# A fused convolution-as-attention and state-space kernel: C products dealt out by sixteen-part patterns, a clip moved from GpSimd into a relu, and tables of hooks reordered

## The chip, the cores and the metric

The kernel runs on one core of a Trainium2 chip. A core has five engines that each run their own list of instructions in order and wait for each other through semaphores: TensorE (PE, with its weight loads shown apart as PEld), VectorE (DVE), ScalarE (ACT), GpSimd (POOL) and SyncE (SP), which here issues the transfers (DMA). The metric is the device time of one execution, in microseconds (us), as the median of three runs.

## The reference

`x` has shape (8, 256, 48, 48), that is 8 images of 256 channels and N = 2304 pixels ("tokens"), in float32. Two layers are added to it, each behind a group norm. The first finds for each pixel the 16 most similar pixels and averages their features; the second is a two-deep chain of selective state-space ("mamba") blocks that scan over the pixels.

```python
# layer 0, per image
feat_pos = tokens @ W.T + bias                      # 256 features, 256 position channels
pos = pos / maximum(norm(pos), 1e-12)
sim = einsum('bnc,bmc->bnm', pos, pos)              # 2304 x 2304
topksim, topkid = top_k(sim, 16)
out = einsum('bnk,bnkc->bnc', softmax(topksim), feat[topkid])
x = x + out
# layer 1, twice (DEPTH = 2), per image: D_INNER = 512, D_STATE = 16, D_CONV = 4
xn = layernorm(xf)
xi, z = split(xn @ in_w.T)
xc = silu(causal_conv4(xi))
dt_r, B, C = split(xc @ xp_w.T)
dt = softplus(dt_r @ dtp_w.T + dtp_b)
# for every pixel t in order:
h = h * exp(dt_t * A) + dt_t * B_t * x_t            # h: 512 x 16 per image
y_t = sum over the 16 states of h * C_t
y = (y + xc * D) * silu(z)
x = x + y @ out_w.T                                 # after the second block
```

## The kernel before

The pixels of an image go in chunks of T = 384, so there are 6 chunks x 2 blocks = 12 *units* per image and 96 in all, one after the other. A unit holds 16 *steps* of 32 inner channels, laid out so that 128 partitions hold 32 channels x 4 groups of states; the other 4 states lie along the free axis. A step has two *parts* of two states each. So a unit has 32 parts, and every part has one scan on VectorE.

A step costs: `make_bx` (GpSimd, dt times x times B, two steps ahead), four `decay` exponentials (ScalarE, into one of two PSUM banks, one part ahead), two scans (VectorE), and the product of the state with C. That product is done by one of two engines, part by part. `on_pool` says which. In a "V" part VectorE makes it, straight after the scan, from the bank `da`; ScalarE then saves the last state and clears a column (`carry`) before the bank is filled again. In a "G" part the scan writes into `bx` and GpSimd makes the product one step later (`pool_part`); if both parts of a step are GpSimd's, one instruction covers them. PE sums the states of four steps (`sum_states`).

```python
    PARTS = Q // HQ            # 2
    STEPS = DI // G            # 16
    HOOKS = PARTS * STEPS      # 32 parts in a unit
    LEAD = 2
    BLOCK = 16
    TOPK = (1, 10)
    PHASE = 6
    # ... cut ...
    def decays(m):
        return banks[m % 2][:, 511 - T : 513 + T]

    def on_pool(unit, i, p):
        if unit["b"] + 1 == B:
            return p == PARTS - 1 and i % J < J - 1
        if TOPK[0] <= unit["at"] < TOPK[1]:
            return p == PARTS - 1 or i % 2 == 0
        return p == PARTS - 1

    def run_scan(m):
        # ... cut ...
        h = g if on_pool(unit, i, p) else da
        nc.vector.tensor_tensor_scan(h, da, g, 0.0, ALU.mult, ALU.add)
        if h is da:
            nc.vector.tensor_tensor(
                bx[:, :, 0:T], da.rearrange("p (q t) -> p q t", q=HQ)[:, :, 1:],
                unit["BC"][1][:, qs], ALU.mult,
            )

    def carry(m):
        # ... cut ...
        if not on_pool(unit, i, p):
            h = decays(m).rearrange("p (q t) -> p q t", q=HQ)
            if unit["c"] + 1 < NCH:
                nc.scalar.copy(h_st[:, unit["d"], i, p * HQ : (p + 1) * HQ], h[:, :, T])
            nc.scalar.copy(h[:, :, 0], zeros)

    def pool_part(n):
        # ... cut ...
        lo = [p for p in range(PARTS) if on_pool(unit, i, p)]
        if not lo:
            return
        qs = slice(lo[0] * HQ, (lo[-1] + 1) * HQ)
        g = unit["bx"][i][:, qs]
        nc.gpsimd.tensor_tensor(g[:, :, 0:T], g[:, :, 1:], unit["BC"][1][:, qs], ALU.mult)
```

The second block of a chunk follows two chunks behind the first. All other work of a unit (layer norm, input projection, the four taps of the convolution, loads, gates, output projection) hangs on the parts by two tables: `between` is called before the scan of a part, `behind` after it, and the number in front is the part, counted from the unit's first (negative ones lie in the units before it). The similarity search of the *next* image runs beside the units as one more stream, `layer0`, that gives a little work per part. Its projections fill the first unit of an image, its blocks of 128 pixels the next nine (16 parts a block), by a third table, `within`. The last image has no such stream.

```python
    for m in range(PARTS * NSTEP - HOOKS + end + 1):
        # ... cut ...
        carry(m - 1)
        decay(m + 1)
        if p == 0:
            make_bx(n + LEAD)
            pool_part(n - 1)
            take_up(n + 1)
        else:
            carry_pool(n - 1)
        for f, unit, args in inner.get(m, ()):      # the table "between"
            f(unit, *args)
        run_scan(m)
        for f, unit, args in outer.get(m, ()):      # the table "behind"
            f(unit, *args)
        # ... cut: then one piece of layer0 of the next image
```

In that stream the norm of the position channels is clipped and turned into its inverse root, by ScalarE's logarithm and exponential and a Newton step on GpSimd:

```python
        def inverse_norm(c):
            rn[c] = small.tile([P, TB], F32, tag="rn", name=f"rn_{b}_{c}")
            rsqrt_start(rn[c], n2[c], 0.0)                                  # ScalarE: Ln, Exp
            rsqrt_end(nc.gpsimd, rn[c], n2[c], 0.0, f"rn_{b}_{c}")          # GpSimd: Newton

            def norm(pn):
                n2[c] = small.tile([P, TB], F32, tag="n2", name=f"n2_{b}_{c}")
                nc.scalar.copy(n2[c], pn)

                nc.gpsimd.tensor_scalar(n2[c], n2[c], 1e-24, None, ALU.max)
```

Of the kernel before, what the change touches and what calls it, by code (L numbers as in the profile page):

```python
# [8 lines left out]
F32 = mybir.dt.float32  # L9
BF16 = mybir.dt.bfloat16  # L10
AF = mybir.ActivationFunctionType
ALU = mybir.AluOpType
# [3 lines left out]
P = 128  # L16
GSIZE = 8
TAKEN = -4.0
FAR = 64.0


@with_exitstack
def tile_conv_preact(
# [18 lines left out]
    nc = tc.nc  # L42
    B, C, N = x.shape
# [11 lines left out]
    G = 32  # L55
    J = P // G
# [3 lines left out]
    PARTS = Q // HQ  # L60
# [4 lines left out]
    BLOCK = 16  # L65
    TOPK = (1, 10)
    PHASE = 6
    JR = 1
    assert N % T == 0 and N % P == 0 and T % P == 0 and NS % (J * HQ) == 0

    const = ctx.enter_context(tc.tile_pool(name="const", bufs=1))
# [13 lines left out]
    nc.vector.tensor_scalar(minus, ident, -FAR, None, ALU.mult)  # L85
    three = const.tile([P, 1], F32, tag="three", name="three")
    nc.gpsimd.memset(three, 3.0)
    ones_mean = const.tile([P, P], F32, tag="ones_mean", name="ones_mean")
    nc.gpsimd.memset(ones_mean, 1.0 / C)
    ones_col = const.tile([P, 1], F32, tag="ones_col", name="ones_col")  # L90
# [60 lines left out]
    def rsqrt_start(r, var, eps):  # L151

        nc.scalar.activation(r, var, AF.Ln, bias=eps)
        nc.scalar.activation(r, r, AF.Exp, scale=-0.5)
# [66 lines left out]
    def layer0(b, left, pool, ps0, alone):  # L221
# [37 lines left out]
        n2, rn = {}, {}  # L259
# [11 lines left out]

        def inverse_norm(c):
            rn[c] = small.tile([P, TB], F32, tag="rn", name=f"rn_{b}_{c}")
            rsqrt_start(rn[c], n2[c], 0.0)
            rsqrt_end(nc.gpsimd, rn[c], n2[c], 0.0, f"rn_{b}_{c}")

        def scale(c):

# [9 lines left out]
        def chunk(c, xn):  # L288
            cs = slice(c * T, (c + 1) * T)
            sq = []  # L290

            def project(ob):
                pp = mm0(T, f"pp_{b}_{c}_{ob}")
                for k in range(CB):
                    nc.tensor.matmul(
                        pp, w0_sb[:, k, C + ob * P : C + (ob + 1) * P], xn[:, k, :],
                        start=(k == 0), stop=(k == CB - 1),
                    )
                return pp

            def features(j):
                pf = mm0(C, f"pf_{b}_{c}_{j}")
                for k in range(CB):
                    nc.tensor.matmul(
                        pf, xn[:, k, j * P : (j + 1) * P], w0_sb[:, k, 0:C],
                        start=(k == 0), stop=(k == CB - 1),
                    )
                return pf

            def norms():  # L310
                pn = mm0(TB, f"pn_{b}_{c}")
                for j in range(TB):
                    for k in range(CB):
                        nc.tensor.matmul(
                            pn[:, j : j + 1], sq[0][:, k, j * P : (j + 1) * P], ones_col,
                            start=(k == 0), stop=(k == CB - 1),
                        )
                return pn

            def position(ob):  # L320
                def use(pp):
                    nc.scalar.activation(
                        pos[:, ob, cs], pp, AF.Identity, bias=b_pos[:, ob : ob + 1]
                    )
                    if ob == CB - 1:
                        sq.append(
                            pool.tile([P, CB, T], F32, tag="x", name=f"sq_{b}_{c}", bufs=3 * more)
                        )
                        nc.scalar.activation(sq[0], pos[:, :, cs], AF.Square)

                return use

            def feature(j):
                return lambda pf: nc.scalar.copy(feat[:, c * TB + j, :], pf)

            def norm(pn):
                n2[c] = small.tile([P, TB], F32, tag="n2", name=f"n2_{b}_{c}")
                nc.scalar.copy(n2[c], pn)

                nc.gpsimd.tensor_scalar(n2[c], n2[c], 1e-24, None, ALU.max)  # L340

            for ob in range(CB):
                step(lambda: project(ob), position(ob))
                yield
            if c > 0:
                inverse_norm(c - 1)
            step(lambda: features(0), feature(0))
            yield
            if c > 0:
                scale(c - 1)  # L350
                yield
            for j in range(1, TB):
                step(lambda: features(j), feature(j))
                yield
            step(norms, norm)

        xn = normalized(0)
# [114 lines left out]
        def finish(t):  # L472
# [11 lines left out]


        within = [
            (15, turn, 1), (11, others, 1), (-8, similar, 1), (-2, keep_similar, 3), (-6, keep_similar, 1),
            (-5, keep_similar, 2), (24, turn_back), (19, weights, 3), (1, top, 1), (16, weigh, 0),
            (-9, similar, 0), (-8, similar, 2), (-9, keep_similar, 0), (22, average), (-5, similar, 4),
            (4, top, 3), (-6, similar, 3), (-3, keep_similar, 4), (0, top, 0), (5, others, 0),  # L490
            (3, top, 2), (7, add_top), (5, others, 2), (11, others, 3), (7, others, 4),
            (14, turn, 0), (17, turn, 2), (15, weights, 0), (17, turn, 3), (15, weights, 1),
            (20, turn, 4), (18, weights, 2), (19, weigh, 1), (21, weigh, 3), (10, invert),
            (19, weigh, 2), (20, weights, 4), (21, weigh, 4), (24, finish),
        ]
        begin = min(part for part, *_ in within)
# [14 lines left out]
    with tc.tile_pool(name="first", bufs=1) as pool0, tc.tile_pool(  # L511
        name="first_ps", bufs=1, space=PSUM
# [234 lines left out]
    def silu_z(unit):  # L747
# [3 lines left out]
        for e in range(DB - 1):  # L751
# [11 lines left out]
             dt=[], dt_d={}, dtx_d={}, dtr={}, dtxr={}, bx={}, y={}, inw={}, dmat={}, taps={}, xi={}, cv={},  # L763
# [8 lines left out]

    def on_pool(unit, i, p):

        if unit["b"] + 1 == B:
            return p == PARTS - 1 and i % J < J - 1
        if TOPK[0] <= unit["at"] < TOPK[1]:
            return p == PARTS - 1 or i % 2 == 0
        return p == PARTS - 1

    def make_bx(n):

# [115 lines left out]
    def leave(unit, cb):  # L898
# [14 lines left out]


    between = [
        (-41, load_v), (-32, variance), (7, in_proj, 5), (17, sum_states, 1), (-21, in_proj, 0),
        (38, out_proj, 0), (-16, in_proj, 3), (-15, taps, 2), (-10, softplus), (24, sum_states, 2),
        (-5, load_rep, "dt", 0), (-11, step_size, 0), (-33, center), (18, load_rep, "dtx", 13), (-21, tap, 0),
        (2, load_rep, "dtx", 5), (-17, tap, 1), (-23, load_in, 1), (-17, tap, 2), (-28, load_in, 2),
        (-16, load_in, 7), (19, gate, 1), (-9, times_x, 1), (-8, load_rep, "dtx", 0), (-4, load_rep, "dtx", 2),  # L920
        (25, load_rep, "dt", 15), (-2, load_rep, "dtx", 3), (1, load_rep, "dt", 3), (0, load_rep, "dtx", 4), (4, load_rep, "dtx", 6),
        (7, load_rep, "dt", 6), (10, load_rep, "dtx", 9), (13, load_rep, "dt", 9), (33, sum_states, 3), (15, load_rep, "dt", 10),
        (5, load_rep, "dt", 5), (17, load_rep, "dt", 11), (20, load_rep, "dtx", 14), (5, load_d, 1), (20, load_d, 2),
        (-33, square), (-15, load_in, 5), (-22, load_in, 0), (21, load_rep, "dt", 13), (-11, step_size, 1),
        (11, load_rep, "dt", 8), (8, in_proj, 6), (-32, root), (9, copy_z, 2), (11, gate, 0),
        (38, out_proj, 1), (-6, load_rep, "dtx", 1), (-4, load_bc, 1), (6, in_proj, 7), (3, in_proj, 4),
        (-13, x_proj), (16, load_rep, "dtx", 12), (-2, times_x, 3), (-11, load_in, 6), (-35, affine),
        (39, leave, 0), (-30, spread_root), (23, load_rep, "dt", 14), (-3, load_rep, "dt", 1), (2, times_x, 2),
        (-16, taps, 1), (-14, taps, 3),
    ]  # L930
    behind = [
        (39, leave, 1), (-32, root_end), (-26, load_in, 3), (-1, load_rep, "dt", 2), (28, gate, 2),
        (6, load_rep, "dtx", 7), (9, load_rep, "dt", 7), (12, load_rep, "dtx", 10), (14, load_rep, "dtx", 11), (-12, split),
        (8, load_rep, "dtx", 8), (-18, in_proj, 2), (-15, load_in, 4), (3, load_rep, "dt", 4), (29, load_d, 3),
        (-14, silu_x), (35, gate, 3), (-35, mean), (-20, taps, 0), (-23, normal),
        (22, load_rep, "dtx", 15), (-15, tap, 3), (-20, in_proj, 1), (-28, scale), (-10, load_bc, 0),
        (10, sum_states, 0), (7, copy_z, 0), (5, load_d, 0), (9, silu_z), (19, load_rep, "dt", 12),
        (8, copy_z, 1), (-10, times_x, 0), (33, load_out),
    ]
    inner, outer, early = {}, {}, []  # L940
    for w, unit in enumerate(units):
# [16 lines left out]
    for m in range(PARTS * NSTEP - HOOKS + end + 1):  # L958
        n, p = divmod(m, PARTS)
# [69 lines left out]
```

## Time and profile before

| what | value |
|---|---|
| time, median of 3 runs | 10485.8 us (10466.35 to 10491.26) |
| profiled execution, span | 10473.1 us |
| mean granted TensorE clock | 0.853 |
| one scan, VectorE | 1.75 us |
| top-k passes, VectorE, four per block of 128 pixels, 144 blocks | 2.54 to 2.55 us each |
| transfers | 1271.49 MB, mean 121 GB/s |

A page of the profile names a group of instructions by its line in the kernel, the engine, the operation, and output<-inputs with their shapes; then the busy time of the group in us, the mean duration of one in ns, and after the second bar the idle time of the engine just before them with what ended it. "L857" is line 857 of the kernel. The answers on waits read: engine, line and tile that waited <- what it waited for: us in total, times, longest. A window line gives start and end, the length, and each engine's busy time with the number of instructions. "issue" is time in which the engine waited for nothing that the profile shows.

### The profile page before, as it was taken

The numbers are of one execution on the slowest core, as the hardware profiler recorded it, in microseconds if no ns is written. First come the engines' busy times: TensorE is split into PE (matmuls) and PEld (weight loads), VectorE is DVE, ScalarE is ACT, GpSimd is POOL, SyncE is SP. The second block draws the span as 40 slices with busy tenths as digits, with TensorE's granted clock in tenths as the row PEclk, the third lists the DMA queues.
The fourth block names the chain that finished last, engine by engine and source line by source line (L and its number), as shares of the span: only waits on it lengthen the run. The fifth ranks groups of instructions, "written<-read, shape, count | busy, mean of one in ns | idle before, by whom it ended". The sixth has DMA issues, their size and how long they took to land.

```text
span 10473.1 us, 135567 instructions
## 1 busy us (share of the span) xinstructions
PE 8225.8 (79%) x36736; PEld 4471.3 (43%) x36736; DVE 9041.7 (86%) x8040; ACT 7506.5 (72%) x17226; POOL 8918.0 (85%) x4142
## 2 busy tenths in 40 slices
PE   8788886888868887788877888678886888866555
PEld 6544443444434444344433444344443444422222
DVE  4589997899979999799987999879998899988898
ACT  4477776777767777677776777767776777766766
POOL 0189997999979999799997999879998899988887
PEclk9888987898878888889887989789897888877777
DMA  1144444444444444444444444444444444444444
GB/s 31 55 111 126 123 131 127 122 123 127 125 134 119 123 126 128 129 120 126 123 129 120 131 125 126 129 123 120 129 127 137 113 128 119 133 130 121 135 132 115
DMA packets 1243516, 1271.49 MB, mean 121 GB/s; under 512 B 266592, under 2 KB 1215840, under 8 KB 1242752
## 3 DMA queue, kind: packets, MB, share of 16 engines
q1 hardware_dynamic: 1230496, 1262.45, 44.3%
q8 instruction: 294, 4.82, 0.2%
q14 instruction: 470, 3.85, 0.1%
q10 hardware_dynamic: 12256, 0.36, 0.1%
HBM read 1048.94 MB, written 212.86 MB: 120 GB/s over the span
## 4 chain that ended last, share of the span: by engine, by line
PE 29%; ACT 25%; DVE 21%; DMA 9%; SPq 9%; issue 6%; POOL 2%; ACTq 0%; DVEq 0%; POOLq 0%
ACT da L812 10%; SPq L559 7%; DVE bx L827 6%; PE psim L385 6%; DVE da L827 5%; PE po L451 5%; DMA dtxr<-dtx_d 4%; PE pe L585 4%; PE y L875 3%; DVE bx L829 2%; PE pw L893 2%; PE pt L431 2%; DVE xc L685 2%; ACT sim L394 2%; DMA dtr<-dt_d 1%
## 5 line engine op out<-in xcount | busy, mean ns | idle before, releaser
L788 POOL TENSOR_TENSOR bx<-BC,dtxr 128x1536 f32<-128x1536 f32 x1536 | 5296.6, 3449 | 268.9 <-PE y L875 190.4
L812 ACT ACTIVATE da<-dtr,A_sb 128x384 f32<-128x384 f32 x6144 | 3585.3, 584 | 630.6 <-DVE bx L827 441.1
L827 DVE TENSOR_TENSOR_SCAN bx<-da,bx 128x770 f32<-128x770 f32 x1992 | 3452.7, 1748 | 283.2 <-ACT da L812 267.8
L857 POOL TENSOR_TENSOR bx<-bx,BC 128x1536 f32<-128x1536 f32 (+1 forms) x1488 | 3260.6, 2191 | 371.3 <-DVE bx L827 273.2
L827 DVE TENSOR_TENSOR_SCAN da<-da,bx 128x770 f32<-128x770 f32 x1080 | 1893.5, 1753 | 251.0 <-ACT da L812 123.4
L385 PE MATMUL psim<-pos 128*128 128x512 f32 (+1 forms) x2880 | 1482.9, 649 | 455.7 <-ACT sim L394 212.4
L585 PE MATMUL pe<-vn,inw 128*128 128x384 f32 (+1 forms) x3072 | 1244.6, 536 | 259.9 <-DMA inw<-in_in_wT_dram 106.8
L451 PE MATMUL po<-feat,aT 128*128 128x256 f32 x5184 | 1315.9, 407 | 1.0
L875 PE MATMUL y<-bx,sel 128*32 128x384 f32 x12288 | 1245.5, 539 | 46.7 <-POOL bx L857 27.5
L451 PEld LDWEIGHTS po<-feat,aT 128*128 128x128 f32 x5184 | 1032.7, 203 | 299.7 <-issue 107.2
L829 DVE TENSOR_TENSOR bx<-da,BC 128x768 f32<-128x768 f32 x1080 | 1035.4, 959 | 37.9 <-DMA BC<-bc_d 0.9
L385 PEld LDWEIGHTS psim<-pos 128*128 128x128 f32 x2880 | 573.2, 212 | 1143.3 <-issue 470.9
L585 PEld LDWEIGHTS pe<-vn,inw 128*128 128x128 f32 x3072 | 609.4, 208 | 727.2 <-issue 178.9
L685 DVE SCALAR_TENSOR_TENSOR xc<-pe,cw,xc 128x384 f32<-128x384 f32 x1152 | 704.4, 612 | 87.5 <-ACT xc L677 60.2
L875 PEld LDWEIGHTS y<-bx,sel 128*32 128x32 f32 x12288 | 391.3, 119 | 899.3 <-issue 764.3
L440 ACT ACTIVATE aT<-pt 128x512 f32<-128x512 f32 (+1 forms) x720 | 396.4, 551 | 489.5 <-PE po L451 269.0
L715 PE MATMUL pd<-dbl,dtp_sb 16*128 16x384 f32 x768 | 443.1, 693 | 306.3 <-ACT dt L724 169.2
L431 PE MATMUL pt<-ident,sim 128*128 128x128 f32 x2592 | 577.2, 307 | 80.7 <-ACT aT L440 39.4
L394 ACT COPY sim<-psim 128x512 f32<-128x512 f32 (+1 forms) x720 | 383.1, 532 | 317.8 <-PE psim L385 316.7
L872 PE MATMUL y<-xc,dmat 128*128 128x384 f32 x768 | 413.5, 627 | 208.8 <-ACT bx L802 108.3
L893 PE MATMUL pw<-z,ow 128*128 128x384 f32 x1536 | 546.1, 510 | 34.5 <-DMA ow<-in_out_wT_dram 10.7
L735 POOL TENSOR_TENSOR dtx<-dt,xc 128x384 f32<-128x384 f32 x384 | 383.8, 1000 | 205.1 <-ACT dt L724 133.3
(147 smaller groups left out, 10053.4 us busy)
## 6 DMA issues: line engine op xcount, KB each, us to landing
dtxr<-dtx_d SPq DMA_DIRECT2D x6144, 48.0 KB, 1.9
dtr<-dt_d SPq DMA_DIRECT2D x6144, 48.0 KB, 1.9
BC<-bc_d SPq DMA_DIRECT2D x768, 192.0 KB, 3.6
inw<-in_in_wT_dram SPq DMA_DIRECT2D x768, 128.0 KB, 2.3
dtx_d<-dtx SPq DMA_DIRECT2D x384, 192.0 KB, 2.0
dt_d<-dt SPq DMA_DIRECT2D x384, 192.0 KB, 2.1
ow<-in_out_wT_dram SPq DMA_DIRECT2D x96, 512.0 KB, 4.2
dmat<-diag SPq DMA_DIRECT2D x384, 64.0 KB, 2.0
```

The lines of the kernel that those rows point to most:

```text
L385: nc.tensor.matmul(pm, pos[:, k, t * P : (t + 1) * P], pos[:, k, c0 : c0 + w], start=(k == 0), stop=(k == CB - 1),)
L431: nc.tensor.transpose(pt[:, q], row["sim"][:, r], ident)
L451: nc.tensor.matmul(row["po"], aT[:, m % PT, :], feat[:, m, :], start=(m == 0), stop=(m == NB - 1))
L585: nc.tensor.matmul(pe, w[:, k], unit["vn"][:, k, lo:], start=(k == 0), stop=(k == CB - 1))
L685: nc.vector.scalar_tensor_tensor(unit["xc"][e], unit["pe"][e][:, k : k + T], cw[:, unit["d"], e, k : k + 1], unit["xc"][e], ALU.mult, ALU.add,
L788: nc.gpsimd.tensor_tensor(bx[:, :, 1:], unit["BC"][0], unit["dtxr"][i // JR][:, i % JR : i % JR + 1, :].to_broadcast([P, Q, T]), ALU.mult,)
L812: nc.scalar.activation(da[:, s * (1 + T) + 1 : (s + 1) * (1 + T)], unit["dtr"][i // JR][:, i % JR, :], AF.Exp, scale=A_sb[:, unit["d"], i, ...
L827: nc.vector.tensor_tensor_scan(h, da, g, 0.0, ALU.mult, ALU.add)
L829: nc.vector.tensor_tensor(bx[:, :, 0:T], da.rearrange("p (q t) -> p q t", q=HQ)[:, :, 1:], unit["BC"][1][:, qs], ALU.mult,)
L857: nc.gpsimd.tensor_tensor(g[:, :, 0:T], g[:, :, 1:], unit["BC"][1][:, qs], ALU.mult)
L875: nc.tensor.matmul(y[j * G : (j + 1) * G, :], sel, unit["bx"][k * J + j][:, q, 0:T], start=False, stop=True, skip_group_check=True,)
L893: nc.tensor.matmul(pw, unit["ow"][:, k, cb * P : (cb + 1) * P], unit["z"][k], start=(k == 0), stop=(k == DB - 1),)
```

## The change

The hand-written rule of `on_pool` is replaced by three patterns of sixteen letters, one for the nine search units, one for the other three units of images 0 to 6, and one for the last image. The pattern repeats every sixteen parts, the same length as a block of the similarity search, so a letter always stands at the same place of a block. The clip of the squared norm no longer needs GpSimd: ScalarE's copy out of PSUM becomes relu(n2 - 1e-24), and 1e-24 is added again where the value is used, which gives the same maximum. The three tables are reordered, and many of their rows move by a part or more, or from one table to the other. The aim is a smoother sharing of work between the engines and fewer waits of GpSimd.

```diff
+TINY = 1e-24
+    SHARE = ("GGVGGGVVGGGGGGVG", "GGGVGVVGVVVGVGVG", "VGVGVGVVGGVVGGVG")
+    tiny = const.tile([P, 2], F32, tag="tiny", name="tiny")
+    nc.gpsimd.memset(tiny[:, 0:1], -TINY)
+    nc.gpsimd.memset(tiny[:, 1:2], TINY)
@@ inverse_norm
-            rsqrt_start(rn[c], n2[c], 0.0)
-            rsqrt_end(nc.gpsimd, rn[c], n2[c], 0.0, f"rn_{b}_{c}")
+            rsqrt_start(rn[c], n2[c], tiny[:, 1:2])
+            rsqrt_end(nc.gpsimd, rn[c], n2[c], TINY, f"rn_{b}_{c}")
@@ norm
-                nc.scalar.copy(n2[c], pn)
-
-                nc.gpsimd.tensor_scalar(n2[c], n2[c], 1e-24, None, ALU.max)
+
+                nc.scalar.activation(n2[c], pn, AF.Relu, bias=tiny[:, 0:1])
@@ on_pool
-        if unit["b"] + 1 == B:
-            return p == PARTS - 1 and i % J < J - 1
-        if TOPK[0] <= unit["at"] < TOPK[1]:
-            return p == PARTS - 1 or i % 2 == 0
-        return p == PARTS - 1
+        stage = 2 if unit["b"] + 1 == B else 0 if TOPK[0] <= unit["at"] < TOPK[1] else 1
+        return SHARE[stage][(i * PARTS + p) % BLOCK] == "G"
```

The tables are long; these are the rows whose part or table changes and that the text speaks of (b = between, h = behind; a row in `within` counts parts of a block):

```
within:   keep_similar 0: -9 -> -8   keep_similar 1: -6 -> -7   keep_similar 3: -2 -> -3
          add_top: 7 -> 6            invert: 10 -> 11           weigh 0: 16 -> 17
          others 1: 11 -> 7          others 3: 11 -> 6          others 4: 7 -> 10
          weigh 1: 19 -> 18          weights 3: 19 -> 21        turn 3: 17 -> 20
          turn 4: 20 -> 18           (top 0 to 3 stay at 0, 1, 3, 4)
per unit: load_v b-41 -> b-42        affine b-35 -> h-37        mean h-35 -> h-37
          center b-33 -> b-35        square b-33 -> b-34        variance b-32 -> b-33
          root b-32 -> b-30          root_end h-32 -> h-30      spread_root b-30 -> b-29
          normal h-23 -> b-22        tap 0: b-21 -> b-20        taps 0: h-20 -> h-19
          step_size 0: b-11 -> h-10  step_size 1: b-11 -> b-10  softplus b-10 -> h-10
          times_x 0: h-10 -> h-9     times_x 1: b-9 -> b-8      times_x 3: b-2 -> h-3
          times_x 2: b2 -> h1        load_d 0: h5 -> b-3        load_in 6: b-11 -> b-17
          sum_states 0: h10 -> b10   sum_states 1: b17 -> h17   sum_states 3: b33 -> h33
          gate 2: h28 -> b29         silu_z h9 -> b9            leave 1: h39 -> h40
```

Other loads of weights and of dt and dtx keep their part or move by one to four, and the order of rows within a part changes throughout.

More of the change, by code (lines that the diff above doesn't have):

```diff
@@ L486, in layer0 @@
         within = [
[L487 to L493, printed above, removed]
+            (21, weights, 3), (4, top, 3), (14, turn, 0), (15, weights, 0), (6, others, 3),
+            (-5, similar, 4), (-8, keep_similar, 0), (-5, keep_similar, 2), (24, turn_back), (18, weigh, 1),
+            (17, weigh, 0), (1, top, 1), (-9, similar, 0), (-8, similar, 1), (-7, similar, 2),
+            (22, average), (-6, similar, 3), (-7, keep_similar, 1), (-3, keep_similar, 3), (0, top, 0),
+            (-3, keep_similar, 4), (15, turn, 1), (10, others, 4), (5, others, 0), (3, top, 2),
+            (6, add_top), (11, invert), (5, others, 2), (17, turn, 2), (20, turn, 3),
+            (15, weights, 1), (18, turn, 4), (18, weights, 2), (21, weigh, 3), (7, others, 1),
             (19, weigh, 2), (20, weights, 4), (21, weigh, 4), (24, finish),
@@ L915, in tile_conv_preact @@
     between = [
[L916 to L929, printed above, removed]
+        (-35, center), (7, in_proj, 5), (24, sum_states, 2), (-33, variance), (-21, in_proj, 0),
+        (-15, taps, 1), (38, out_proj, 0), (-15, taps, 2), (-14, taps, 3), (-34, square),
@@ new lines, in tile_conv_preact @@
+        (39, leave, 0), (23, load_rep, "dt", 14), (5, load_rep, "dt", 5), (-4, load_bc, 1), (38, out_proj, 1),
+        (17, load_d, 2), (-17, tap, 1), (18, load_rep, "dtx", 13), (-8, times_x, 1), (19, gate, 1),
+        (-22, normal), (1, load_rep, "dt", 3), (0, load_rep, "dtx", 4), (15, load_rep, "dt", 10), (6, load_rep, "dtx", 7),
+        (10, load_rep, "dtx", 9), (12, load_rep, "dtx", 10), (20, load_rep, "dtx", 14), (11, gate, 0), (-29, spread_root),
+        (-19, load_in, 5), (33, load_out), (-22, load_in, 0), (21, load_rep, "dt", 13), (-20, tap, 0),
@@ new lines, in tile_conv_preact @@
+        (-10, step_size, 1), (9, copy_z, 2), (-18, in_proj, 2), (2, load_rep, "dtx", 5), (10, sum_states, 0),
+        (13, load_rep, "dt", 9), (29, gate, 2), (9, silu_z), (7, load_rep, "dt", 6), (19, load_rep, "dt", 12),
+        (-6, load_rep, "dtx", 1), (-14, load_in, 7), (-30, root), (9, load_rep, "dt", 7), (4, load_d, 1),
+        (-24, load_in, 3), (17, load_rep, "dt", 11), (14, load_rep, "dtx", 11), (-13, x_proj), (-17, load_in, 6),
+        (-3, load_d, 0), (4, load_rep, "dtx", 6), (-4, load_rep, "dtx", 2), (-42, load_v),
@@ L930, in tile_conv_preact @@
     ]
     behind = [
[L932 to L936, printed above, removed]
@@ L937, in tile_conv_preact @@
-        (10, sum_states, 0), (7, copy_z, 0), (5, load_d, 0), (9, silu_z), (19, load_rep, "dt", 12),
-        (8, copy_z, 1), (-10, times_x, 0), (33, load_out),
+        (-12, split), (-3, load_rep, "dt", 1), (3, in_proj, 4), (-10, step_size, 0), (-5, load_rep, "dt", 0),
+        (-8, load_rep, "dtx", 0), (-15, tap, 3), (-1, load_rep, "dt", 2), (-28, scale), (16, load_rep, "dtx", 12),
+        (11, load_rep, "dt", 8), (8, in_proj, 6), (17, sum_states, 1), (-14, silu_x), (25, load_rep, "dt", 15),
@@ new lines, in tile_conv_preact @@
+        (-37, affine), (1, times_x, 2), (7, copy_z, 0), (8, load_rep, "dtx", 8), (-17, tap, 2),
+        (-10, softplus), (-16, in_proj, 3), (3, load_rep, "dt", 4), (-29, load_in, 2), (6, in_proj, 7),
+        (35, gate, 3), (-2, load_rep, "dtx", 3), (8, copy_z, 1), (40, leave, 1), (-3, times_x, 3),
+        (22, load_rep, "dtx", 15), (-16, load_in, 4), (29, load_d, 3), (-37, mean), (-19, taps, 0),
+        (-19, in_proj, 1), (-10, load_bc, 0), (33, sum_states, 3), (-30, root_end), (-9, times_x, 0),
@@ L939, in tile_conv_preact @@
+        (-22, load_in, 1),
     ]
```

## The prediction

> **What bounds the kernel now.** I read the page first (engine shares, chain, groups), then cut the span where the work changes, then took the waits of each stretch.
>
> ```profile
> PE 8225.8 (79%) x36736; PEld 4471.3 (43%) x36736; DVE 9041.7 (86%) x8040; ACT 7506.5 (72%) x17226; POOL 8918.0 (85%) x4142
> ...
> PE 29%; ACT 25%; DVE 21%; DMA 9%; SPq 9%; issue 6%; POOL 2%; ACTq 0%; DVEq 0%; POOLq 0%
> ...
> L788 POOL TENSOR_TENSOR bx<-BC,dtxr 128x1536 f32<-128x1536 f32 x1536 | 5296.6, 3449 | 268.9 <-PE y L875 190.4
> L812 ACT ACTIVATE da<-dtr,A_sb 128x384 f32<-128x384 f32 x6144 | 3585.3, 584 | 630.6 <-DVE bx L827 441.1
> L827 DVE TENSOR_TENSOR_SCAN bx<-da,bx 128x770 f32<-128x770 f32 x1992 | 3452.7, 1748 | 283.2 <-ACT da L812 267.8
> L857 POOL TENSOR_TENSOR bx<-bx,BC 128x1536 f32<-128x1536 f32 (+1 forms) x1488 | 3260.6, 2191 | 371.3 <-DVE bx L827 273.2
> L829 DVE TENSOR_TENSOR bx<-da,BC 128x768 f32<-128x768 f32 x1080 | 1035.4, 959 | 37.9 <-DMA BC<-bc_d 0.9
> ```
>
> No engine is full over the span: VectorE and GpSimd are near 86%, and the chain passes between PE, ACT and DVE, with 2% on POOL. An average over unlike stages hides what matters, so I cut it. There are 96 units (8 images, 6 chunks, 2 layers) of 32 parts; every part has one scan, so unit k begins at scan 32k of VectorE's timeline. The first scan starts at 490.4 us (before it the first image's similarity search runs alone), images 0 to 6 take 1260 to 1268 us each, the last image 1142. Within an image the first unit takes 144 us on average, the next nine (similarity search of the following image beside them) 102.9 each, the last two 100.4 and 92.9; a unit of the last image takes 95.2. The windows, image 3 standing for images 0 to 6 (columns: PE, PEld, DVE, ACT, POOL busy, clock, DMA share, GB/s):
>
> ```profile
> 0.00:490.40 490.40, 423.71 (x1997) 301.60 (x1998) 235.18 (x255) 211.97 (x433) 24.09 (x78) 0.95 0.12 32
> 4273.70:4420.00 146.30, 110.95 (x465) 65.12 (x464) 93.85 (x92) 91.48 (x219) 96.12 (x98) 0.82 0.43 124
> 4420.00:5348.10 928.10, 789.46 (x3608) 434.98 (x3607) 854.84 (x749) 705.60 (x1607) 871.07 (x342) 0.89 0.46 124
> 5348.10:5541.40 193.30, 126.83 (x526) 59.75 (x525) 165.41 (x150) 133.62 (x306) 170.66 (x85) 0.75 0.49 132
> 9331.00:10473.10 1142.10, 666.50 (x2655) 283.36 (x2654) 1009.21 (x874) 777.96 (x1885) 931.75 (x412) 0.73 0.46 126
> ```
>
> In the nine search units GpSimd is busy 94% (871.1 of 928.1) and VectorE 92%: two engines at their limit together, with 57.0/9 = 6.3 us of GpSimd idle per unit. In the first unit nothing is above 76%: waits bound it. In the last two VectorE and GpSimd are at 86% and 88%, in the last image at 88% and 82%. The waits of three stretches (the first unit; the last two; the last image):
>
> ```profile
> POOL n L340 <- ACT n L338: 27.4, 5, 14.2
> PE pm_a L181 <- DVE mv_a L178: 14.9, 1, 14.9
> DVE st L249 <- DMA xs<-in_x_dram: 11.4, 4, 6.1
> DVE z L881 <- PE y L875: 11.1, 1, 11.1
> ...
> DVE da L827 <- ACT da L812: 11.4, 5, 4.6
> POOL bx L857 <- DVE bx L827: 10.6, 5, 3.9
> ...
> ACT h_st L844 <- DVE bx L829: 176.8, 128, 2.8
> POOL bx L857 <- DVE bx L827: 134.6, 72, 4.9
> ```
>
> **What the Trainium skill says.** *Perfetto Trace Analysis*, section "Optimization Strategy", asks to take each regime by itself when the most-contended engine changes, and to look at the gaps on that engine; the windows agree that it changes. *GPSIMD Engine Reference*, "Engine selection", calls GpSimd about twice as slow as VectorE for two-input elementwise work; here the same 128x768 product takes 1683 ns on GpSimd (groups kept apart by shape) against 959, 1.75 times. *SBUF — State Buffer*, "Who interferes with whom", says that a VectorE instruction with two SBUF inputs contends with a GpSimd instruction that reads SBUF. The VectorE product reads da from PSUM and BC from SBUF, one SBUF input, so moving products should not slow them; the trace agrees (956 to 962 ns over 1080). *ScalarE: Activation LUTs*, "What ACT_TABLE_LOAD costs", gives 1283 ns for a switch of table set; the trace has 1283 ns too, and its 576 loads are all at the silu and softplus lines, none at the Relu that already runs on the search rows. The new Relu should bring none.
>
> **The change part by part.**
>
> *The shares.* I counted the letters. Search units: the first pattern has 12 G in 16, that is 24 parts in 32, as before. Other units: 8 in 16, again as before. Last image: 8 in 16, where before 12 in 32 parts were GpSimd's. So only the last image's shares move; elsewhere the order does. Two G in one step make one 128x1536 instruction of 3184 ns instead of two of 1683, a saving of 182 ns. Search units go from 8 wide and 8 narrow to 10 wide and 4 narrow: 8 x 3.184 + 8 x 1.683 = 38.9 us becomes 10 x 3.184 + 4 x 1.683 = 38.6, or 0.36 us a unit, 23 us over 63 units if GpSimd were the only limit. The other units gain two wide pairs, 0.36 us of GpSimd again.
>
> *What order can do.* A V part frees its da bank only after the VectorE product, and ScalarE must then save the state (158 ns), clear a column (163 ns) and make two exponentials (2 x 584) before the scan two parts on: 1.49 us, hidden under the part between. If that part is G, VectorE fills only its scan of 1.75 us, 0.26 us over; if V, 1.75 + 0.96. V followed by G is the tight case. Counted per 16 parts, it goes from 4 to 3 in search units, 8 to 5 in the others, 6 to 6 in the last image. The four top-k passes of about 2.54 us fall on the same places of every sixteen parts (6, 7, 9 and 10, counted from 0); where VectorE is thus late, the pattern gives GpSimd no product to wait for (VV at 6 and 7).
>
> Search units: floor GpSimd, 96.9 us busy of 102.9. In this stage GpSimd waits for VectorE's scans only 7.3 us in 9 units and 14.9 for PE to free bx; VectorE waits 22.2 for ScalarE and 16.8 for y. These are spread over engines, so I let the new order return a quarter of the 6.0 us, 1.5, with the 0.36 included, and round up: 63 x 1.6 = 100 us.
>
> Last two units of images 0 to 6: 11.4 us of scan waits in two units, 5.7 each; five eighths of the tight places remain, which would return 2.1, and the saving of wide pairs is off the path: 14 x 2.3 = 32 us.
>
> Last image: 4 parts per unit leave VectorE, 4 x 0.96 = 3.8 us; GpSimd goes from 12 x 1.683 = 20.2 to 4 x 3.184 + 8 x 1.683 = 26.2, that is 6.0 more, from 77.4 busy to 83.4 of 95.2, using its 134.6 us of waiting. VectorE goes from 84.2 to 80.4. I count 60% of 3.8: 12 x 2.3 = 28 us.
>
> *The norm clip.* It removes 48 GpSimd instructions of 226 ns (10.9 us) and, on paper, 218 us of waits before them. But in the first unit, while GpSimd stood 14.2 us, ScalarE was working through silu, z and norm work and VectorE was waiting 11.1 us for y; the chain of that unit has no GpSimd piece. GpSimd's next wait, for the exponential of the same norm, stays. ScalarE pays nothing but a pointer bias on a 162 ns copy. I count 3 us of 144 per unit: 7 x 3 = 21 us.
>
> *The tables.* The layer norm starts earlier (affine and mean -35 to -37, center -33 to -35, root -32 to -30), which lengthens the distance between its links; `load_d 0` moves from 5 to -3; softplus and `times_x` fall one part later. PE waits hang on these (v to lm, lsq to lv), but PE is not the floor. I give the tables no sum of their own, and take 30 us off for transfers or buffers that now collide.
>
> Sum: 100 + 32 + 28 + 21 - 30 = 151; 10485.8 - 151 = 10335, which I put at 10330.
>
> **The rivals.** First, *nothing moves*: shares are equal in 84 of 96 units, and the waits are scattered over PE, ScalarE and DMA, so closing one opens the next. For it: chain with 2% on POOL. It would leave the last image alone, 10440 to 10480. Second, *the coupling was the loss*: GpSimd and VectorE run in order, each waiting for the other, and smoothing returns more than half of 6.0 us in search units and the clip's full 27 us in first units: 63 x 3.5 + 7 x 15 + 60 = 386, or 10100. Against it: GpSimd's waits for scans are small in search units. Third, *the tables hurt*: ScalarE's order moves in 144 blocks and 96 units, the table loads and exponentials collide, and scans wait more; 1 us a unit gives 10580. Fourth, the clock: PE runs at 0.89 in search units and lower in others; a denser schedule may lower it, which would eat gains where y is awaited.
>
> **Range and chances.** The first rival sets the upper side, half of the second the lower: 10180 to 10470. More than 2% faster means below 10276, 210 us, which needs the search units to give over 2.5 us each; I give it 0.25. Slower by 2%, 10696, would need 2 us lost in every unit: 0.05. Within 2%: 0.70.
>
> **What would show it.** Right: product groups of 3.18 and 1.68 us unchanged, 14 product instructions in a search unit, the unit at 101 to 102 us, GpSimd busy above 95%; last-image units near 93; VectorE products down by 48; the wait at the clip gone, first units down by less than 5 us. Wrong: first units 10 us or more shorter (the clip did gate), search units under 100 (coupling), or a wait of scans for ScalarE, or of PE for its psum buffers, that grew.

## The result and the profile after

The changed kernel takes 10089.5 us (10084.76 to 10093.57, six runs) against 10482.8 before (10466.35 to 10491.26, now six runs as well): ratio 0.9626, 95% interval 0.9613 to 0.9638. That is 393 us, where the sum of the prediction came to 151; the time lies below the predicted range.

The page of the changed kernel (same form as the page of before; line numbers have moved):

```profile
PE 8011.2 (79%) x36736; PEld 4387.2 (44%) x36736; DVE 8971.1 (89%) x7992; ACT 7487.2 (74%) x16998; POOL 8944.0 (89%) x3928
...
L791 POOL TENSOR_TENSOR bx<-BC,dtxr 128x1536 f32<-128x1536 f32 x1536 | 5301.9, 3455 | 81.4 <-PE y L878 37.8
...
L830 DVE TENSOR_TENSOR_SCAN bx<-da,bx 128x770 f32<-128x770 f32 x2040 | 3525.2, 1747 | 191.8 <-ACT da L815 142.3
L860 POOL TENSOR_TENSOR bx<-bx,BC 128x1536 f32<-128x1536 f32 (+1 forms) x1320 | 3306.5, 2505 | 253.2 <-DVE bx L830 235.7
...
L832 DVE TENSOR_TENSOR bx<-da,BC 128x768 f32<-128x768 f32 x1032 | 989.1, 958 | 35.5
```

The busy times have hardly moved: VectorE 70 us less, GpSimd 26 us more. The durations of one scan and one product are the same. What went is idle time: before `make_bx` GpSimd stood 268.9 us, now 81.4. The chain of waits on this page covers only a tenth of the span, so I don't read it. The same five windows as before (image 3 for images 0 to 6):

```profile
0.00:501.80 501.80, 431.97 (x1998) 299.82 (x1998) 235.17 (x255) 213.25 (x433) 22.72 (x73) 0.95 0.12 32
4145.60:4283.60 138.00, 106.52 (x466) 63.42 (x467) 93.35 (x92) 93.03 (x217) 89.87 (x89) 0.83 0.44 130
4283.60:5170.60 887.00, 762.02 (x3609) 424.42 (x3608) 852.23 (x749) 704.85 (x1591) 867.83 (x324) 0.93 0.46 130
5170.60:5357.00 186.40, 120.63 (x521) 56.73 (x519) 164.84 (x151) 132.51 (x303) 174.00 (x82) 0.77 0.47 136
8999.10:10083.00 1083.90, 654.20 (x2647) 279.42 (x2646) 964.06 (x826) 761.61 (x1797) 999.06 (x412) 0.75 0.46 133
```

The nine search units go from 928.1 to 887.0 us while GpSimd's work goes from 871.1 to 867.8: it is now busy 98% of this stage. So 41.1 us of the stage are gone, and only 3.2 of them are work. What GpSimd waits for in these nine units (engine, line and tile <- what it waited for: us, times, longest), before:

```profile
POOL bx L788 <- PE y L875: 14.9, 11, 3.0
POOL bx L788 <- DMA dtr<-dt_d: 9.0, 4, 4.0
POOL dtx L735 <- ACT dt L724: 7.3, 9, 1.4
POOL bx L857 <- DVE bx L827: 7.3, 13, 1.5
POOL dtx L735 <- issue: 5.3, 7, 0.8
```

and after, all of it:

```profile
POOL bx L860 <- DVE bx L830: 12.5, 12, 1.7
POOL bx L791 <- PE y L878: 3.6, 3, 1.6
POOL bx L791 <- ACT da L815: 2.4, 1, 2.4
POOL bx L791 <- ACT xc L699: 0.5, 1, 0.5
```

Four of the five waits shown have gone or shrunk to crumbs. The fifth, for VectorE's scans (`L857 <- L827` before, `L860 <- L830` after), has grown from 7.3 to 12.5 us and is most of what is left.

This table gives mean unit lengths of every run, counted from scan 32k on VectorE's timeline as in the prediction ("start" is the time of the first scan; 1st, search, 11th and 12th are the units of images 0 to 6; "last" is a unit of the last image), with the run's ratio to the kernel before. The unit lengths come from one profiled execution of each kernel.

| kernel | start | 1st | search (9) | 11th | 12th | last | ratio (95%) |
|---|---|---|---|---|---|---|---|
| before | 490.4 | 143.9 | 102.9 | 100.4 | 92.9 | 95.2 | 1 |
| after | 501.8 | 140.5 | 98.6 | 95.4 | 90.9 | 90.3 | 0.9626 (0.9613-0.9638) |
| e1 patterns | 489.6 | 141.6 | 101.9 | 98.5 | 92.2 | 92.8 | 0.9896 (0.9880-0.9911) |
| e2 all tables | 501.6 | 145.4 | 98.9 | 99.0 | 90.8 | 94.2 | 0.9754 (0.9738-0.9770) |
| e3 relu | 490.4 | 143.8 | 102.8 | 100.1 | 93.1 | 95.1 | 0.9995 (0.9986-1.0003) |
| e4 after, pattern turned | 502.0 | 140.6 | 100.1 | 95.8 | 90.8 | 90.2 | 0.9727 (0.9712-0.9741) |
| e5 within | 498.6 | 143.2 | 101.4 | 99.5 | 93.0 | 95.1 | 0.9910 (0.9893-0.9927) |
| e6 between, behind | 491.3 | 145.6 | 100.6 | 99.3 | 91.1 | 94.1 | 0.9850 (0.9835-0.9864) |
| e7 dtx 0, 1 later | 488.3 | 144.3 | 103.0 | 100.0 | 92.6 | 94.8 | 1.0005 (0.9996-1.0013) |
| e8 half similarity | 446.9 | 143.6 | 102.5 | 100.7 | 92.7 | 94.9 | 0.9934 (0.9919-0.9949) |
| e9 weights 3 later | 510.9 | 144.4 | 103.3 | 99.7 | 93.0 | 95.1 | 1.0041 (1.0026-1.0055) |
| e10 layer norm rows | 491.4 | 141.1 | 103.2 | 100.1 | 92.0 | 95.0 | 0.9991 (0.9983-1.0000) |
| e11 projection to dtx | 489.6 | 148.5 | 100.4 | 100.8 | 91.2 | 94.5 | 0.9875 (0.9861-0.9890) |
| e12 load rows | 490.2 | 145.1 | 102.8 | 101.1 | 93.9 | 94.8 | 1.0003 (0.9996-1.0009) |
| e13 dt rows | 491.3 | 147.4 | 101.1 | 100.3 | 92.7 | 94.9 | 0.9908 (0.9892-0.9925) |
| e14 projection, taps | 489.9 | 146.9 | 102.0 | 100.0 | 91.2 | 94.7 | 0.9947 (0.9932-0.9962) |
| e15 turn, weigh rows | 495.7 | 143.6 | 102.0 | 99.0 | 92.9 | 95.2 | 0.9948 (0.9933-0.9962) |
| e16 copies, relus | 488.2 | 142.8 | 102.1 | 100.2 | 93.2 | 94.9 | 0.9949 (0.9934-0.9964) |
| e17 after, old clip | 499.8 | 140.1 | 98.6 | 95.4 | 91.0 | 90.4 | 0.9636 (0.9613-0.9659) |
| e18 after, old start | 490.9 | 140.4 | 98.6 | 95.4 | 91.0 | 90.6 | 0.9633 (0.9614-0.9652) |

The stages of before minus after make up the whole: 63 x 4.3 (search) + 7 x 3.4 (first) + 7 x (5.0 + 2.0) + 12 x 4.9 - 11.4 (start) = 271 + 24 + 49 + 59 - 11 = 392, where the two profiled spans differ by 390.1.

### The profile page after: what moved, and what is told of

Its sections match the earlier page's. It is cut to its first block, busy times and chain, and to the rows that moved or that the text cites. A ratio compares the mean times of both kernels' runs of the same rounds, so it can differ in the third digit from the quotient of the medians.

```text
span 10083.0 us, 134837 instructions
## 1 busy us (share of the span) xinstructions
PE 8011.2 (79%) x36736; PEld 4387.2 (44%) x36736; DVE 8971.1 (89%) x7992; ACT 7487.2 (74%) x16998; POOL 8944.0 (89%) x3928
## 5 line engine op out<-in xcount | busy, mean ns | idle before, releaser
L791 POOL TENSOR_TENSOR bx<-BC,dtxr 128x1536 f32<-128x1536 f32 x1536 | 5301.9, 3455 | 81.4 <-PE y L878 37.8
L830 DVE TENSOR_TENSOR_SCAN bx<-da,bx 128x770 f32<-128x770 f32 x2040 | 3525.2, 1747 | 191.8 <-ACT da L815 142.3
L860 POOL TENSOR_TENSOR bx<-bx,BC 128x1536 f32<-128x1536 f32 (+1 forms) x1320 | 3306.5, 2505 | 253.2 <-DVE bx L830 235.7
L830 DVE TENSOR_TENSOR_SCAN da<-da,bx 128x770 f32<-128x770 f32 x1032 | 1810.9, 1755 | 247.0 <-ACT da L815 161.8
L391 PE MATMUL psim<-pos 128*128 128x512 f32 (+1 forms) x2880 | 1377.8, 611 | 203.0 <-ACT sim L400 88.5
L457 PE MATMUL po<-feat,aT 128*128 128x256 f32 x5184 | 1358.1, 411 | 21.2 <-ACT aT L446 14.9
L832 DVE TENSOR_TENSOR bx<-da,BC 128x768 f32<-128x768 f32 x1032 | 989.1, 958 | 35.5
L691 DVE SCALAR_TENSOR_TENSOR xc<-pe,cw,xc 128x384 f32<-128x384 f32 x1152 | 696.3, 611 | 37.6 <-ACT xc L683 10.4
L721 PE MATMUL pd<-dbl,dtp_sb 16*128 16x384 f32 x768 | 417.5, 658 | 340.9 <-ACT dt L730 171.2
L847 ACT COPY h_st<-da 128x2 f32<-128x2 f32 x832 | 131.6, 158 | 589.7 <-DVE bx L832 582.7
L437 PE MATMUL pt<-ident,sim 128*128 128x128 f32 x2592 | 533.3, 288 | 43.0 <-DVE v L655 18.5
L429 ACT ACTIVATE rest<-left,three 128x512 bf16<-128x512 f32 (+1 forms) x720 | 467.0, 670 | 59.8 <-DVE left L414 59.8
```

The costliest lines, as they stand in the source:

```text
L391: nc.tensor.matmul(pm, pos[:, k, t * P : (t + 1) * P], pos[:, k, c0 : c0 + w], start=(k == 0), stop=(k == CB - 1),)
L437: nc.tensor.transpose(pt[:, q], row["sim"][:, r], ident)
L457: nc.tensor.matmul(row["po"], aT[:, m % PT, :], feat[:, m, :], start=(m == 0), stop=(m == NB - 1))
L691: nc.vector.scalar_tensor_tensor(unit["xc"][e], unit["pe"][e][:, k : k + T], cw[:, unit["d"], e, k : k + 1], unit["xc"][e], ALU.mult, ALU.add,
L791: nc.gpsimd.tensor_tensor(bx[:, :, 1:], unit["BC"][0], unit["dtxr"][i // JR][:, i % JR : i % JR + 1, :].to_broadcast([P, Q, T]), ALU.mult,)
L832: nc.vector.tensor_tensor(bx[:, :, 0:T], da.rearrange("p (q t) -> p q t", q=HQ)[:, :, 1:], unit["BC"][1][:, qs], ALU.mult,)
```

## The experiments

**e1 to e4: which part of the change, and does the place of the letters matter.** My theory was that the patterns make the gain, the rival that the tables do.

```diff
e1, on before:  + SHARE and the new on_pool
e2, on before:  + the tables within, between and behind of the change
e3, on before:  + relu in norm, TINY in inverse_norm, - the clip on GpSimd
e4, on after:   -"GGVGGGVVGGGGGGVG"   +"GGGGGGVGGGVGGGVV"
```

> The kernel before with the three patterns of the change alone; tables and clip as before. Theory A (the order of G and V within sixteen parts makes the gain): at least 60% of the 393 us return here, 10090 to 10250, and search units fall from 102.9 to 100.5 or less. Theory B (the tables make it): the last image falls by some 40 us and little else, 10410 to 10450. Theory C (each needs the other): below both shares, 10350 to 10450, with search units between 101.5 and 103.

> The kernel before with the three tables of the change alone; shares by the old rule and the clip on GpSimd. Theory A (patterns): 10380 to 10480, search units above 101.5. Theory B (tables): 10150 to 10250, search units below 100, GpSimd's wait for PE before make_bx gone from 2.0 us a unit to under 0.7. Theory C (each needs the other): about 10350 to 10450 as in the run with the patterns alone, so that the two gains together fall short of 393 us by over 100.

> The kernel before with the clip alone moved into the relu. My step: first units shorter by about 3 us each, 21 us in all, 10450 to 10475. Rival (the clip gated the first units): 7 units shorter by 10 us or more, 10380 to 10420. Third: the wait only moves to the next GpSimd instruction that needs the norm, 10480 to 10490 and first units at 144.

> The changed kernel with the pattern of the search units turned by eight parts (VGGGGGGVGGGVVGGG... counted from its ninth letter): same number of G, of pairs, of V before G; only the place against the top-k passes differs. If the place against the top-k passes matters, search units go back to 101 or more, which is 150 us over the changed kernel, 10240 or more. If only the number of pairs and of V before G matters, search units stay within 0.5 us of 98.6 and the time within 30 us of 10090.

(The diff has the letters that ran in e4; those in the expectation are miswritten.) The patterns alone return 1.0%, the tables alone 2.5%, the relu nothing that can be measured. In search units the tables give 4.0 of the 4.3 us; the patterns give 1.0 alone and only 0.3 on top of the tables. Theory A falls. e1 by itself would fit theory C (10369.6 us, search units 101.9), and lies below the 10410 to 10450 of B: the patterns return 108 us, in the last image (95.2 to 92.8), the search units and the first units. But e2 returns 261 us, as B said, and 108 + 261 = 369 is only 24 short of 393, so C falls too. B holds for the search units; in the last image the patterns give most. B also had GpSimd's wait for PE before `make_bx` right. In nine search units of e2 it is, against 14.9 us before,

```profile
POOL bx L788 <- PE y L875: 3.2, 6, 0.5
```

The time of e3, 10469.5 us, lies in the range of "my step", but by luck: the kernel before took 10477.6 beside it, the interval of the ratio includes 1, and the first units stay at 143.8. The relu did not free GpSimd: in the first unit of image 3 of e3

```profile
POOL nv_rn L165 <- ACT n L343: 15.3, 3, 8.0
POOL nt_rn L166 <- ACT rn L158: 6.5, 6, 1.9
POOL nv_rn L165 <- ACT h_st L847: 4.4, 1, 4.4
```

and in that of the changed kernel

```profile
POOL nv_rn L168 <- ACT h_st L847: 17.6, 2, 10.3
POOL nt_rn L169 <- ACT rn L161: 10.4, 6, 3.3
```

GpSimd stands about as long, 26.2 us in e3 and 28.0 in the changed kernel (with a third wait of 4.7, 32.7) against 27.4 at the clip before (with 4.0 at the Newton step, 31.4), one instruction further on, at the Newton step that needs the same norm.

e4 shows that the place of the letters does count: a search unit is 1.5 us longer, at 100.1, and the time 10190.1 us. That lies between the two forecasts (101 or more if the top-k passes matter, within 0.5 of 98.6 if not), and the cause is another. Turning the pattern moves it against all work that repeats every sixteen parts, not against the top-k passes alone. With the pattern turned by eight parts GpSimd's waits in nine search units are led by

```profile
POOL bx L860 <- DVE den L422: 24.5, 8, 4.3
POOL bx L791 <- PE y L878: 3.7, 7, 0.5
```

`den` is only the last thing that VectorE did before the product could start. The timeline of one of these eight waits shows what held it:

```profile
4579.22 3.73 DVE L691 SCALAR_TENSOR_TENSOR xc<-pe,cw,xc 128x384 f32<-128x384 f32 x6
4582.87 1.75 DVE L830 TENSOR_TENSOR_SCAN bx<-da,bx 128x770 f32<-128x770 f32 x1
4584.53 0.14 DVE L422 RECIPROCAL den<-den 128x1 f32<-128x1 f32 x1
4584.76 3.18 POOL L860 TENSOR_TENSOR bx<-bx,BC 128x1536 f32<-128x1536 f32 x1 [4.03 <-DVE den L422]
```

Six taps of the convolution (L691) stand in front of the scan, at the same part of every block. The turned pattern has its two V in a row (VV) just before that part: VectorE has two products more to do there, and GpSimd none. Over the 63 search units GpSimd waits 2.5 us a unit for VectorE behind these taps and not at all behind top-k passes. In the changed kernel it is the other way round: 1.2 us behind top-k passes, none behind taps. So the waits that e4 brings stand at the taps, not at the top-k passes. And the hand-written rule had no such fault: with the new tables it stands at 98.9 (e2). The pattern avoids a loss that the old rule did not have either.

**e5, e6, e8: which table, and is it PE.**

```diff
e5, on before:  + the table within of the change
e6, on before:  + the tables between and behind of the change
e8, on before, in similar:  -for k in range(CB):   +for k in range(1):
```

> The kernel before with the table of the similarity blocks (within) alone replaced; the two tables of the units, shares and clip as before. With all tables the search units went from 102.9 to 98.9. Theory D (PE was held by the psum buffers of the similarity stream, y came late and GpSimd waited for bx): at least 2.5 of the 4.0 us return here, search units 100.4 or less, and the whole near 10310. Theory E (the unit tables, above all the dtx products one part later): at most 1.2 us here, 101.7 or more, 10400 or more.

> The kernel before with the two unit tables (between and behind) alone replaced. Theory D: search units at 101.5 or more. Theory E: 100.5 or less. If both this and the run with within alone give under 1.2 us, the gain needs both.

> The kernel before with half of the similarity left out (one of the two channel halves is not multiplied), so that PE has about 6 us less per search unit and nothing else changes in order. Theory F (PE, busy 87 of 103 us, was the hidden third limit: it delivers late): search units fall by 2 us or more. Theory G (the order of waits, not the amount of PE work): by less than 1 us.

Neither D nor E alone: within gives 1.5 us a search unit, the unit tables 2.3, and 3.8 is close to the 4.0 of both. Theory F falls: e8 leaves out half of the similarity, which takes 4.2 us of PE's busy time out of a search unit (87.4 to 83.1; the granted clock is lower too, 0.82 against 0.85 over the span), and a search unit loses 0.4 us; 43 us of its gain are in the first image, which runs alone.

**e7, e9: one wait taken away by itself.**

```diff
e7, on before:  -(-10, times_x, 0)  -(-9, times_x, 1)   +(-9, times_x, 0)  +(-8, times_x, 1)
e9, on before:  -(19, weights, 3)   +(21, weights, 3)
```

> The kernel before with two rows moved: the first two dtx products of GpSimd one part later. GpSimd waited 0.9 us a search unit for dt and 0.65 more just before these products. If those waits are on the path of a stage in which GpSimd is busy 94%, search units fall by 1 to 1.6 us, 60 to 100 us in all, 10380 to 10420. If GpSimd only waits elsewhere instead, the time stays at 10460 to 10490.

> The kernel before with one row of within moved: ScalarE's fourth group of weights of a block from part 19 to 21, so that it no longer stands in front of the PE work that frees its buffer. In the kernel before ScalarE stood 4.3 us a search unit there. If this one wait is what the table within gained, search units fall by 1.0 to 1.5 us (102.9 to 101.4 to 101.9), 60 to 95 us in all; if it is covered, by less than 0.4 us.

Both gave nothing, e9 even cost 0.4%, of which 20.5 us come before the first scan. The waits of GpSimd in nine search units in e7:

```profile
POOL bx L788 <- PE y L875: 22.4, 15, 4.0
POOL bx L857 <- DVE bx L827: 13.9, 13, 1.8
POOL dtx L735 <- ACT dt L724: 9.1, 9, 1.4
```

The "issue" wait before dtx (5.3 us) is gone, but the wait for dt is no smaller than before, and those for PE and for VectorE grew from 14.9 and 7.3. In e9 ScalarE no longer waits for PE to free the weights (40.0 us in nine units before, its longest wait). It waits in their place for the transposes, which went from 15.3 to 61.6:

```profile
ACT aT L440 <- PE pt L432: 61.6, 40, 5.4
```

A wait is not a cost that can be subtracted; the engine is early or late, and the next thing it needs is not there either.

**e10 to e16: which rows.** Each takes the rows named from the change and leaves the others of its tables as before. In e10 to e14 the rows taken stand at the head of their table, so within a part they are called first.

```diff
e10: load_v, affine, mean, center, square, variance, root, root_end, spread_root, scale, normal
e11: in_proj, tap, taps, silu_x, x_proj, split, step_size, softplus, times_x, load_bc
e12: load_in, load_rep, load_d, load_out
e13: step_size, softplus, times_x
e14: in_proj, tap, taps, silu_x, x_proj, split
e15: turn, weights, weigh
e16: similar, keep_similar, others, add_top, invert
```

> The kernel before with the rows of the layer norm alone as in the change (load_v to normal). The two unit tables together gave 2.3 us a search unit. Theory H (the links of the layer norm, in which VectorE waited 0.7 us for ScalarE's square of the root and PE for affine and square): at least 1 us a search unit here. Theory I (the dt chain, softplus to dtx): under 0.4 us here.

> The kernel before with the rows of projection, convolution, step size, softplus and dtx alone as in the change. Theory I: at least 1 us a search unit here. Theory H: under 0.4 us. If neither this nor the layer norm rows give 0.7 us, the gain lies in the loads or in sums and gates, or needs several at once.

> The kernel before with the rows of the loads (inw, dt, dtx, dmat, ow) alone as in the change. Few waits for transfers stand in the profile (under 1.2 us a search unit on GpSimd and VectorE together), so under 0.5 us a search unit, 10450 to 10490; a gain over 1 us would mean that the profile puts waits for transfers down to other engines.

> The kernel before with only step size, softplus and dtx rows as in the change. Theory J (the dt chain): most of the 2.5 us a search unit, 1.5 or more, 10340 to 10390. Theory K (projection and taps): under 0.7 us, 10430 or more.

> The kernel before with only the rows of projection and convolution taps as in the change. Theory K: 1.5 us a search unit or more, 10340 to 10390. Theory J: under 0.7 us. If both are under 1 us the two groups need each other.

> The kernel before with only the rows turn, weights and weigh of within as in the change. Theory L (ScalarE stood 4.3 us a search unit for the buffer of weights; moved together with its transposes the wait goes and stays away): at least 1 us of the 1.5 a search unit, and the first image some 10 us longer. Theory M (earlier copies and relus): under 0.4 us, and the first image at 490.

> The kernel before with only the rows of similarity, its copies, the relus and the top sum as in the change. Theory M: at least 1 us of the 1.5 a search unit. Theory L: under 0.4 us. If both are under 0.7, they need each other.

Layer norm and loads: nothing in search units. Projection to dtx (e11): 2.5, all that the unit tables give there. It splits into 1.8 (e13, theory J) and 0.9 (e14). Within splits into 0.9 (e15) and 0.8 (e16): neither L nor M alone. Four groups, 1.8 + 0.9 + 0.9 + 0.8 = 4.4, together 4.0 in e2: they nearly add up. In times they do: 0.92 + 0.53 + 0.52 + 0.51 = 2.48% against 2.46% in e2. e13 beside e7 shows what a whole link does and one row does not. In e13 step size, softplus and all four dtx products move together, and of GpSimd's two waits before dtx (7.3 and 5.3 us before) neither is left among those of nine search units; these lead:

```profile
POOL bx L788 <- PE y L875: 19.8, 13, 3.9
POOL bx L857 <- DVE bx L827: 12.7, 17, 1.1
POOL bx L857 <- DMA inw<-in_in_wT_dram: 2.3, 3, 0.9
```

The dt rows leave the order of ScalarE's instructions, and of VectorE's, as it was (the sequences in the two traces are equal); they move PE's step-size products and GpSimd's dtx. All the same VectorE's waits for ScalarE's exponentials before a `bx` scan fell from 2.4 to 1.1 us a search unit (summed over the 63 units). Through which wait the one causes the other was not tried.

**e17, e18: the first units and the start.**

```diff
e17, on after:  the clip of before, with 0.0 in inverse_norm
e18, on after, in layer0:  + if alone: within = [the table of before]
```

> The changed kernel with the clip back on GpSimd. If the relu matters once the tables are new, first units are 3 us or more longer than 140.5, 20 to 35 us in all, 10110 to 10130. If it does not (as in the kernel before, where it moved the time by 0.05%), within 8 us of 10090.

> The changed kernel with the old table of blocks for the first image, which runs alone. The first scan starts at 490 instead of 501.8 us and the rest stays, 10070 to 10085. If the 11 us come from elsewhere, the time stays at 10090.

The old clip in the changed kernel: 10086.8 us (10084.23 to 10088.6), first units 140.1. So the 4.9 us between e2 and the changed kernel there (145.4 to 140.5) are the patterns', not the relu's. The start: before the first scan VectorE waits for ScalarE's sum of the top values, before

```profile
DVE den L416 <- ACT top L413: 33.0, 17, 2.0
```

and in the changed kernel

```profile
DVE den L422 <- ACT top L419: 44.2, 17, 3.1
```

11.2 us more, as much as the start is late (11.4). With the old table for this image alone (e18) the start is back at 490.9 and this wait at 32.9, so the table within is the cause. That this one wait carries it is not shown: in e16 it is 41.7 us too, and the start is not late (488.2); in e15 the start is 5 us late without it, and in e9, which moves `weights 3` alone as the change does, it is 20.5 us late without it. The rows of e15 alone bring 5.3 us, those of e16 none, both together 8.2 (e5), and all tables 11.2 (e2); how they combine is open. The time of e18 is 10084.7 us (10080.59 to 10086.15), 5 us under the median of the changed kernel, but the two intervals of the ratio overlap. The profiled span fell by only 4.1 us, so most of the 10.9 us won at the start were lost later, and that e18 is faster than the changed kernel is not shown.

## Why the prediction was wrong

*Search units.* The step that failed is the sentence "I let the new order return a quarter of the 6.0 us", and with it "I give the tables no sum of their own". The floor was right: GpSimd's 96.8 us became 96.4, by the 0.4 us of wide pairs. The term was mis-sized: 4.3 us a unit came back instead of 1.6, 271 us instead of 100. The letters, for which the 1.6 was meant, return 1.0 alone; the tables, which got nothing, return 4.0. I took waits spread over several engines as a sign that closing one opens the next. e7 and e9 show that this holds for one wait at a time, and e2, e5, e6, e13 to e16 that it does not hold for whole groups of rows: four of them return 0.8 to 1.8 us each, and the returns add. Two smaller readings were wrong as well: only `times_x` 0 and 1 move later, 2 and 3 come earlier; and VV at 6 and 7 does not keep GpSimd from waiting behind the top-k passes, where 1.2 us a unit are left.

*The first rival*, that nothing moves, fell for the same reason; *the second*, that more than half of the 6.0 us return, has the right size here (3.9 of 6.0 on GpSimd) with the wrong cause: neither the clip nor the smoothing by patterns, but the tables. *The third* fell, but for the start (11 us). *The clock*: it did not sink but rose, 0.89 to 0.93 in search units.

*The clip.* I predicted 21 us; e3 and e17 measure none. The reading that it was not on the path was right, and so was the sentence that GpSimd's next wait stays; the 3 us a unit booked in spite of that had no ground. First units did become 3.4 us shorter, but the number came out by luck. The patterns did it, for which the prediction had no term there: they take 2.3 us off alone (e1) and 5.3 on top of the tables (e2 to e17), which alone cost 1.5. The relu itself took 262 ns where the copy took 162.

*Last image.* Predicted 2.3 us a unit, measured 4.9. The work moved as reckoned, GpSimd to 83.3 us busy a unit and VectorE to 80.3. e1, where only the patterns change, gives 2.4: the step of 60% of 3.8 us is right. Tables alone give 1.0, both together 4.9, so 1.5 comes only with both.

*Last two units.* Predicted 2.3 each, measured 5.0 and 2.0, 49 us instead of 32. Patterns alone give 1.9 and 0.7, tables 1.4 and 2.1. Whether the count of V before G did it was not tried by itself.

*Collisions.* The 30 us taken off came as 11 us at the start and, with the tables alone, as 1.5 us in each first unit.

*The range.* Its lower end, 10180, was called half of the second rival. It allows 306 us, four fifths of that rival's 386; half would have ended at 10293.

## What to carry to other kernels

Here two engines were each busy over 90% of a stage, their remaining idle time was scattered in small waits, and reordering won 3.9 of the 6.0 us between the stage and the busier engine's work: that gap, not the largest wait, was the measure of what could be won. Moving one or two rows only moved a wait, while moving a whole link of a chain (step size, softplus and the products behind it) closed it, and the returns of such groups added up. A table tuned for work that runs beside other work need not suit that work where it runs alone: it started 11 us later here. And the engine named in a wait can be the last of several things in the way; e4 is read rightly only from the timeline.

## What was not expected of the hardware

The granted TensorE clock rose from 0.853 to 0.883 over the span with the same 36736 matmuls (e2 0.882, e1 0.865, e3 0.853). It does not follow the time alone: e9 is slower than the kernel before and has 0.867, and e15 and e16 take the same time (10422.8 and 10426.4 us) at 0.868 and 0.853. No run here separates cause from effect, but e9 shows that a higher clock came without a gain. The products on VectorE and GpSimd's `make_bx` kept their durations over the span (959 to 958 and 3449 to 3455 ns; in the nine search units `make_bx` went from 3455 to 3468) although both engines were busy more of the time, so no added contention of more than 0.4% shows in these means.
